# Marks that DVE and ACT write, turned into integer rows by GpSimd

## The chip, the cores and the metric

The program runs on one core of a Trainium2 chip. The metric is device time in microseconds (us) of one execution. The engines are PE (TensorE), DVE (VectorE), ACT (ScalarE), POOL (GpSimd) and SP (SyncE, which here only issues DMAs). Each engine works through its own queue in order. POOL both computes and issues the indirect DMAs, and while it issues one it can do nothing else.

## The reference

The input x has 4 x 2048 = 8192 tokens of 256 features. It is normalised (layernorm), and two branches work on the result. The first is a gated linear recurrence: a projection, a scan over time of an 8-wide state, and an output projection; it gives s. The second is a mixture of experts with 32 experts; it gives g. The result is x + s * silu(g). What matters here is how a token gets its place at an expert:

```python
scores = softmax(xf @ wg.T)                  # 32 experts in 8 groups of 4
# the best 4 groups are kept; of their experts the best K = 4 take the token
pos  = (jnp.cumsum(oh, axis=0) * oh).sum(-1) - 1     # its turn at that expert
keep = pos < cap                                     # cap = 1280 places an expert
dest = jnp.where(keep, fe * cap + pos, E * cap)
xe   = xp[buf_tok].reshape(E, cap, DIM)              # the rows that each expert gets
h    = silu(xe @ w1) * (xe @ w3);  out = (h @ w2) * buf_w
y    = zeros.at[buf_tok].add(out);  z = (silu(xf @ sw1) * (xf @ sw3)) @ sw2
g    = y + z
```

## The kernel before

**First stage: routing and shared work.** The tokens are taken in nine batches, r = 0 to 8: two of 512 tokens and seven of 1024. A batch lies in a tile `xt` of 128 partitions with 4 or 8 tokens on each. For each batch the kernel normalises it (`norm`), turns it by PE (`to_features`), computes the logits, picks the experts (`choose`), counts the places (`count`, `place`), and writes token number and weights beside the features (`weigh`). `place` leaves in the tile `t8` the row numbers, as floats, of each token's four places in a buffer `xd_d` in device memory. Between these steps lie the dense "shared" expert (`shared_hidden`, `shared_out`), the recurrence (`recur`, a scan on DVE in line 414) and its projection.

**Dispatch.** `dispatch(r, t8)` writes the rows as integers into a tile `put` and sends the tokens to their rows. It makes groups: 4 in batches 0 and 1, 8 in each later batch, 64 in all. A group is one small copy of 128 x 4 numbers from `t8` to `put` (line 595; the copy to another type is called a CAST in the profile), and behind it four indirect DMAs on POOL (`send`, line 546), each of which scatters 128 rows. The groups are not all emitted at once: they stand in the list `waiting`, and `go_on` emits one here and there among the other work, on DVE in most places (50 groups) and on ACT in some (14). In the last batch the groups go by column: the first two hold column 3 of all 1024 tokens, the next two column 2, and so on. A token's rows are sorted, so expert 0 can only be in column 3, expert 1 in columns 2 and 3, and so on.

**The order of the work.** The regions are under `manual_schedule(engines=engines)` with PE, DVE, ACT and SP: these four issue in the order in which the program emits. POOL is not among them. A planner orders POOL's queue, by what is ready in its own model and then by the order of emission.

**Second stage: the experts.** For each expert e, SP loads its rows from `xd_d` in tiles of 128 rows (`load_slots`, line 797, with a register load ahead of each); for experts 0 to 3 the first tile of each span waits for the scatters of the columns that can hold this expert (line 805 on). Rows go through PE (`turn`), `first_blocks`, `second_blocks`, then `hidden`, a seven-product scheme in which DVE writes the tile `h` in line 873 (its part `c`) and ACT in line 878; then `down` multiplies with w2, ACT scales (line 917) and POOL adds the rows to `y_d` by an indirect DMA (line 918). The two last blocks of the shared expert are written to `y_d` by POOL (line 619), the others by SP.

**Memory.** Tiles come from pools. `put` lies in the pool `keep`, which lives to the end. `t8`, with the rest of routing's small tiles, lies in the pool `rt`, two buffers of each name. The pools `ab`, `xp`, `rt` and `sh` of the first stage are given back at its end, and the second stage's pools `fin`, `moe`, `arms` and so on are laid from the same first byte. They are made with `reuse_waits="tile"`: a new tile waits for whoever still uses an earlier tile on its own bytes, and for nobody else. `h` is in `arms`.

**End.** The last stage loads `y_d`, applies silu, multiplies with s, adds x and writes the output.

Of the kernel before, what the change touches and what calls it, by code (L numbers as in the profile page):

```python
# [8 lines left out]
F32 = mybir.dt.float32  # L9
# [7 lines left out]
def recurrent_moe_kernel(  # L17
# [18 lines left out]
    nc = tc.nc  # L36
    P = 128
# [5 lines left out]
    K = 4  # L43
# [10 lines left out]
    RT = 8  # L54
# [72 lines left out]
    def go_on(n=1, copy=nc.vector.tensor_copy):  # L127
        for _ in range(min(n, len(waiting))):
            waiting.pop(0)(copy)
# [36 lines left out]
    with tc.tile_pool(name="ab", bufs=1) as ab, tc.tile_pool(name="xp", bufs=4) as xp, tc.tile_pool(  # L166
        name="rt", bufs=2
# [353 lines left out]
        def place(r, M, cum, pc):  # L521

            n = RTS[r]
            base = rt.tile([P, E], F32, tag="base", name=f"base_{r}")
            nc.vector.tensor_tensor(base, pc[:, 1, :], carry, ALU.add)
            nc.vector.tensor_tensor(carry, pc[:, 0, :], carry, ALU.add)
            ejs = [P, E, n]
            pos = by_expert("pos", r)
            nc.vector.tensor_tensor(pos, cum, base.unsqueeze(2).to_broadcast(ejs), ALU.add)
            over = by_expert("ml", r)  # L530
            nc.vector.tensor_scalar(over, pos, 0.0, 1.0e6, ALU.max, ALU.mult)
            nc.vector.tensor_tensor(pos, pos, eoff.unsqueeze(2).to_broadcast(ejs), ALU.add)
            nc.vector.tensor_tensor(pos, pos, over, ALU.add)
            sl = wide("sl", r)
            nc.vector.tensor_tensor(sl.rearrange("p j e -> p e j"), pos, M, ALU.mult)
            t8 = wide("t8", r, 8)
            for j in range(n):
                nc.vector.max(t8[:, j, :], sl[:, j, :])
            go_on(len(waiting))
            nc.vector.tensor_scalar(t8[:, :n, 0:K], t8[:, :n, 0:K], gone, None, ALU.min)  # L540
            return t8
# [3 lines left out]
        def send(index, rows, column):  # L545
            ins = nc.gpsimd.indirect_dma_start(  # L546
                out=xd_d,
                out_offset=bass.IndirectOffsetOnAxis(ap=index, axis=0),
                in_=rows,
                in_offset=None,  # L550
            )
            apart("xd", ins)
            sent.append((column, ins.ins.name))
            if column is not None:
                tc.add_to_no_dep_group(f"column{column}", ins.ins)
# [32 lines left out]
        def dispatch(r, t8):  # L588


            put = keep.tile([P, RT, K], I32, tag="put", bufs=2, name=f"put_{r}")
            final = r + 1 == NR

            def group(js, ks, copy):
                copy(put[:, js, ks], t8[:, js, ks])
                for j in range(js.start, js.stop):
                    for k in range(ks.start, ks.stop):
                        send(put[:, j, k : k + 1], xts[r][:, j, :], k if final else None)

            for i in range(RTS[r]):  # L600
                if final:
                    k, j = K - 1 - i // 2, i % 2 * K
                    waiting.append(lambda copy, a=slice(j, j + K), b=slice(k, k + 1): group(a, b, copy))
                else:
                    waiting.append(lambda copy, a=slice(i, i + 1): group(a, slice(0, K), copy))
            go_on(1 if 2 < r < NR - 1 else 2)
# [44 lines left out]
        put = place(0, M, cum, pc)  # L651
        weigh(0, M, ex)
        dispatch(0, put)
        load_x(3)
        gate_bias()
# [12 lines left out]
        put = place(1, M, cum, pc)  # L668
        weigh(1, M, ex)
        dispatch(1, put)  # L670
        load_x(4)
        to_features(2, 0, first=True)
# [14 lines left out]
        put = place(2, M, cum, pc)  # L687
        weigh(2, M, ex)
        dispatch(2, put)
        hT = shared_hidden(1)  # L690
        load_x(5)
# [17 lines left out]
        put = place(3, M, cum, pc)  # L709
# [14 lines left out]
        for r in range(4, NR + 1):  # L724
# [24 lines left out]
            if new:  # L749
                pc = count(r, cum)  # L750
                put = place(r, M, cum, pc)
# [374 lines left out]
```

## Time and profile before

| | |
|---|---|
| median of 3 runs | 1130.21 us (1129.55 to 1130.8) |
| profiled execution, its own time | 1130.25 us |
| span of its trace | 1128.4 us |
| PE busy | 1046.4 us of the span |
| POOL busy | 699.0 us |
| DVE busy | 700.1 us |
| ACT busy | 506.0 us |
| scatters of line 546 | 256, from 29.7 to 373.5 us |
| first row load of an expert (line 797) | 348.35 us |

The span runs from the first to the last instruction; 1.85 us of the execution lie around it. A line of the trace's timeline gives start, duration, engine, source line, operation, output and inputs, their shapes, and in brackets the idle time of the engine just before it and what ended it ("issue": nothing that the profile shows). A number such as x2 says that neighbouring instructions of one kind are merged. SPq, POOLq and so on are an engine's sequencer: it waits or issues, and the engine itself is idle.

### The profile page before, as it was taken

Reading aid. Unit: us, or ns where it says so; the run is one execution under the profiler, and the core shown is the slowest. Engines: PE = TensorE matmul, PEld = TensorE weight load, DVE = VectorE, ACT = ScalarE, POOL = GpSimd, SP = SyncE. Lnnn points to the kernel's source line nnn. Section 1 sums busy time; section 2 is a strip of 40 time slices with the busy share of each in tenths; the row PEclk is TensorE's granted clock in tenths of the full one; section 3 lists DMA queues with packets and bytes.
Section 4 is the critical chain, followed back from the end, with each engine's and each line's share of the span. In section 5 each row is a group of like instructions: output and inputs, shape, how many; then the busy total and the mean of one; then the engine's idle time right before and its main releaser. Section 6 shows DMA issues by size and latency. Waiting matters only on the chain.

```text
span 1128.4 us, 16045 instructions
## 1 busy us (share of the span) xinstructions
PE 1046.4 (93%) x3882; PEld 652.6 (58%) x3882; DVE 700.1 (62%) x1950; ACT 506.0 (45%) x990; POOL 699.0 (62%) x562
## 2 busy tenths in 40 slices
PE   6799899999999999999999999999999999999930
PEld 3366466566666566665566556665665665665620
DVE  6887786786542556555565555565555655655567
ACT  2355345534532444444444444444444444444442
POOL 2777777777777654566545655565566466466470
PEclk9999999999999999999999999999999999999975
DMA  6363443533368887777877887788777878778599
GB/s 212 125 204 124 166 156 135 186 132 146 130 207 260 211 192 155 156 143 182 173 169 161 167 204 164 135 175 192 148 153 171 188 157 190 170 148 166 99 255 388
DMA packets 149837, 197.28 MB, mean 175 GB/s; under 512 B 17706, under 2 KB 133331, under 8 KB 149715
## 3 DMA queue, kind: packets, MB, share of 16 engines
q0 software_dynamic: 53184, 79.07, 35.5%
q1 hardware_dynamic: 95922, 116.50, 34.1%
q8 instruction: 48, 0.79, 0.3%
q14 instruction: 75, 0.61, 0.2%
q10 hardware_dynamic: 608, 0.31, 0.1%
HBM read 99.05 MB, written 96.76 MB: 174 GB/s over the span
## 4 chain that ended last, share of the span: by engine, by line
PE 61%; DMA 2%; DVE 1%; issue 1%; POOL 0%; ACT 0%; SPq 0%; ACTq 0%; DVEq 0%; POOLq 0%
PE eo L915 20%; PE ps L867 19%; PE ps L870 14%; PE ep L842 5%; PE xu L102 3%; DMA out_dram<-xr 1%; DMA y<-y_d 1%; DVE y L1084 1%; PE xh L974 0%; PE xp L957 0%; DVE xr L1085 0%; POOL out_dram L1087 0%; POOL y_d L918 0%; ACT y L1083 0%; ACT ob L917 0%
## 5 line engine op out<-in xcount | busy, mean ns | idle before, releaser
L918 POOL DMA_INDIRECT y_d<-ob,row x274 | 424.0, 1547 | 293.5 <-DVE rf L816 200.4
L546 POOL DMA_INDIRECT xd_d<-xt,put x256 | 262.5, 1025 | 102.8 <-issue 61.5
L915 PE MATMUL eo<-w,h 128*128 128x256 f32 x1024 | 237.1, 379 | 0.3 <-DVE h L880 0.3
L915 PEld LDWEIGHTS eo<-w,h 128*128 128x128 f32 x1024 | 188.5, 190 | 31.3 <-issue 8.8
L917 ACT ACTIVATE ob<-eo,wt 128x256 f32<-128x256 f32 x274 | 118.9, 471 | 130.0 <-PE eo L915 130.0
L867 PE MATMUL ps<-B,S 128*128 128x512 f32 x384 | 175.3, 592 | 1.3 <-DVE B L858 1.3
L873 DVE TENSOR_TENSOR u<-p,ps 128x512 f32<-128x512 f32 x64 | 44.0, 687 | 186.6 <-PE ps L867 186.6
L870 PE MATMUL ps<-B,w 128*128 128x512 f32 x256 | 130.7, 592 | 0.0
L867 PEld LDWEIGHTS ps<-B,S 128*128 128x128 f32 x384 | 72.9, 190 | 93.4 <-issue 77.2
L893 ACT COPY ps<-v 128x512 f32<-128x512 f32 x64 | 37.7, 589 | 120.3 <-DVE v L873 120.3
L870 PEld LDWEIGHTS ps<-B,w 128*128 128x128 f32 x256 | 48.0, 189 | 61.9 <-DVE ps L873 31.2
L842 PEld LDWEIGHTS ep<-ident,xe 128*128 128x128 f32 x512 | 59.9, 141 | 20.2 <-DMA xe<-xd_d 9.8
L878 ACT ACTIVATE h<-ps 128x512 f32<-128x512 f32 x96 | 53.8, 595 | 30.7 <-PE ps L870 30.7
L102 PE MATMUL po<-Wio,xnT 128*128 128x256 f32 x256 | 66.8, 384 | 0.2 <-ACT zt L616 0.2
L842 PE MATMUL ep<-ident,xe 128*128 128x128 f32 x512 | 66.5, 273 | 0.3 <-ACT B L850 0.3
L867 PE MATMUL ps<-B,w 128*128 128x512 f32 x128 | 66.0, 597 | 0.6 <-DVEq L993 0.3
L870 PE MATMUL ps<-B,S 128*128 128x512 f32 x128 | 66.0, 598 | 0.1
L880 DVE TENSOR_TENSOR h<-h,ps 128x512 f32<-128x512 f32 x96 | 62.9, 682 | 3.3 <-PE ps L870 0.2
L102 PE MATMUL pz<-sw,hT_s 128*128 128x256 f32 x256 | 60.7, 390 | 0.4 <-DVE hT_s L142 0.4
L102 PE MATMUL pa_s<-xnT,sw 128*128 128x512 f32 x128 | 60.9, 598 | 0.0
L102 PE MATMUL pb_s<-xnT,sw 128*128 128x512 f32 x128 | 60.1, 592 | 0.0
L102 PEld LDWEIGHTS po<-Wio,xnT 128*128 128x128 f32 x256 | 48.4, 193 | 10.4 <-issue 3.8
(173 smaller groups left out, 1400.9 us busy)
## 6 DMA issues: line engine op xcount, KB each, us to landing
xe<-xd_d SPq DMA_DIRECT2D x320, 144.5 KB
w<-in_L_ffn_w_dram SPq DMA_DIRECT2D x96, 256.0 KB
xt<-in_L_attn_x_dram SPq DMA_DIRECT2D x16, 512.0 KB
xr<-in_L_attn_x_dram SPq DMA_DIRECT2D x16, 512.0 KB
y<-y_d SPq DMA_DIRECT2D x16, 512.0 KB
y_d<-zt SPq DMA_DIRECT2D x14, 512.0 KB
y_d<-ob,row POOLq DMA_INDIRECT x274, 4.9
xd_d<-xt,put POOLq DMA_INDIRECT x256, 2.7
```

Of the source, the lines that this page charges most:

```text
L102: nc.tensor.matmul(ps, lhsT, rhs, start=(i == 0), stop=(i == len(pairs) - 1))
L546: ins = nc.gpsimd.indirect_dma_start(out=xd_d, out_offset=bass.IndirectOffsetOnAxis(ap=index, axis=0), in_=rows, in_offset=None,)
L842: nc.tensor.transpose(ps[:, j * P : (j + 1) * P], xes[e, i][:, j, k * P : (k + 1) * P], ident)
L867: nc.tensor.matmul(ps[n], a, b, start=True, stop=True)
L870: nc.tensor.matmul(ps[n], a, b, start=False, stop=True, skip_group_check=True)
L873: nc.vector.tensor_tensor(to, a, b, ALU.add)
L878: nc.scalar.activation(h[:, m, t], src, AF.Silu)
L880: nc.vector.tensor_tensor(h[:, m, t], h[:, m, t], src, ALU.mult)
L893: nc.scalar.copy(ps[2], v)
L915: nc.tensor.matmul(po[:, i, :], hT(m), ws[e][:, 2, m, :], start=(m == 0), stop=(m == KH - 1))
L917: nc.scalar.activation(ob[:, q % 2, :], po[:, i, :], AF.Copy, scale=wts[e][:, q : q + 1])
L918: ins = nc.gpsimd.indirect_dma_start(out=y_d, out_offset=bass.IndirectOffsetOnAxis(ap=rows[e][:, q : q + 1], axis=0), in_=ob[:, q % 2, :], ...
```

## The change

`dispatch` gets a tile of floats, `mark`, from the pool `rt`. The copy that DVE or ACT makes for a group now goes from `t8` to `mark`, float to float. Behind it, POOL itself copies the group from `mark` to `put`, float to integer, and then issues the group's four scatters, which read `put` as before. The tile `put`, the scatters and all other work are the same.

```diff
@@ dispatch(r, t8)
             put = keep.tile([P, RT, K], I32, tag="put", bufs=2, name=f"put_{r}")
             final = r + 1 == NR
 
+            mark = rt.tile([P, RT, K], F32, tag="mark", name=f"mark_{r}")
+
             def group(js, ks, copy):
-                copy(put[:, js, ks], t8[:, js, ks])
+                copy(mark[:, js, ks], t8[:, js, ks])
+                nc.gpsimd.tensor_copy(put[:, js, ks], mark[:, js, ks])
                 for j in range(js.start, js.stop):
                     for k in range(ks.start, ks.stop):
                         send(put[:, j, k : k + 1], xts[r][:, j, :], k if final else None)
```

## The prediction

> **What bounds the kernel now.** I read the page's engine shares and chain first, then the busy table by stretches, then the timelines of POOL, SP, DVE and ACT around the change of stage.
>
> ```profile
> PE 1046.4 (93%) x3882; PEld 652.6 (58%) x3882; DVE 700.1 (62%) x1950; ACT 506.0 (45%) x990; POOL 699.0 (62%) x562
> 192.00:342.00 150.00, 143.55 (x552) 94.61 (x551) 96.67 (x398) 66.33 (x93) 115.88 (x112) 1.00 0.48 159
> 342.00:376.00 34.00, 32.04 (x112) 19.18 (x111) 11.91 (x22) 11.23 (x23) 24.77 (x27) 1.00 0.86 274
> ```
>
> The stretches list length, then PE, PEld, DVE, ACT, POOL. PE is full in both (143.55 of 150, 32.04 of 34), so POOL's 62% over the whole looks harmless. But POOL's own timeline says otherwise:
>
> ```profile
> 156.27 0.96 POOL L546 DMA_INDIRECT xd_d<-xt,put  x1 [0.30 <-issue]
> 158.67 1.27 POOL L546 DMA_INDIRECT xd_d<-xt,put  x1 [1.45 <-DVE put L595]
> 166.49 0.96 POOL L546 DMA_INDIRECT xd_d<-xt,put  x1 [1.72 <-DVE put L595]
> 192.31 0.95 POOL L546 DMA_INDIRECT xd_d<-xt,put  x1 [0.82 <-DVE put L595]
> 341.50 0.96 POOL L546 DMA_INDIRECT xd_d<-xt,put  x1 [0.30 <-issue]
> 367.83 0.59 POOL L619 DMA_DIRECT2D y_d<-zt  x1
> 368.73 0.99 POOL L546 DMA_INDIRECT xd_d<-xt,put  x1 [0.30 <-DVE h L873]
> ```
>
> A scatter lasts 0.96 and the next starts 0.30 later: one per 1.26 us, 5.05 a group. From 29.7 us to the end POOL really waits for a row copy in three places only, by 1.45, 1.72 and 0.82, of which 0.30 each is the usual gap: 3.1 us of slack. After 192.31 there is none: POOL's queue is a backlog, and whatever is added to it moves its end. The last copy is made by DVE at 353.78, its scatters start at 368.73, 15 us later. So the question is who waits for POOL around 340 to 380.
>
> ```profile
> 348.35 8.75 SPq L797 DMA_DIRECT2D xe<-xd_d  x8
> 353.78 0.17 DVE L595 CAST put<-t 128x4 int32<-128x4 f32 x1
> 367.95 0.69 DVE L873 TENSOR_TENSOR h<-v,ps 128x512 f32<-128x512 f32 x1 [0.17 <-PE ps L867]
> 368.81 0.60 ACT L878 ACTIVATE h<-ps 128x512 f32<-128x512 f32 x1 [0.35 <-PE ps L870]
> ```
>
> Here is expert 0's first load, which waits for column 3 (its last scatter is the 341.50 one), and the two first writes of `h`.
>
> **The price of a copy on POOL, c.** No row shows such a copy. The nearest are POOL's small operations at the start:
>
> ```profile
> 1.07 0.15 POOL L203 IOTA eoff<- 128x32 f32 x1
> 1.18 0.28 POOL masks.py:199 TENSOR_SCALAR_AFFINE_SELECT ident<-ident 128x128 f32<-128x128 f32 x1
> 1.43 0.28 POOL L199 TENSOR_SCALAR_AFFINE_SELECT tri<-tri 128x128 f32<-128x128 f32 x1
> 1.95 0.16 POOL L215 IOTA at<- 128x10 f32 x1
> 2.06 0.14 POOL L218 IOTA gone<- 128x1 f32 x1
> ```
>
> From below: short operations follow each other at 0.11 (1.95 to 2.06), less than their records, since they overlap. From above: the DMA of line 619 puts 0.59 between two scatters, and it is a whole DMA issue. Nearest is an operation that reads and writes, 0.25 from start to start for 128 numbers (1.18 to 1.43); for 4 numbers it must be nearer the short record of 0.16, but the scatter waits for its end, so nothing overlaps. I take 0.20. The 0.30 ahead of the scatter doesn't come twice: at 192.31 the scatter starts 0.28 after the end of the DVE copy that it waited for, as it would behind its own engine.
>
> A rule of the Trainium skill speaks against this change (SBUF — State Buffer, "SBUF: two separate sides"): DVE and GpSimd share one port pair as an exclusive lock, and a DVE operation with two SBUF inputs, or in a two-port mode, shuts a reading GpSimd operation out until it ends. The row first:
>
> ```profile
> 320.78 1.65 POOL L546 DMA_INDIRECT xd_d<-xt,put  x1 [0.30 <-issue]
> 322.74 2.02 POOL L546 DMA_INDIRECT xd_d<-xt,put  x1 [0.30 <-DMA xd_d<-hole]
> 321.64 2.34 DVE L414 TENSOR_TENSOR_SCAN St<-Gt,St,St 8x1024 f32<-8x1024 f32 x1
> ```
>
> While the scan runs, scatters take 1.65 and 2.02 in place of 0.96: the lock is real here. Were every DVE operation such a lock, a copy would meet one with 64% (96.67 of 150 us) and wait some 0.3 us for it (my estimate: mean operation 96.67 / 398 = 0.24, long ones are met more often), c would be 0.4 and the sum below +22. But all 256 scatters together are at a mean of 1.025 against 0.96, so the whole lock costs 0.065 for an operation five times as long; for a copy that is 0.01 to 0.07. I stay with 0.20.
>
> **Part by part.**
> 1. DVE's 50 and ACT's 14 copies stay: casts of 128x4 take 0.16 and 0.19, and the float copies nearest to them (line 813, 128x10 on DVE, 0.16; line 823, 128x4 on ACT, 0.19) the same. Zero. Their waits for `put` of two batches earlier (28 semaphore instructions on each of the two queues, 0.05 and 0.04 us) move to POOL, where the sequencer already takes 64 such during the scatter before without a gap over 0.30. Zero; without that cover 28 x 0.05 = 1.4 us on POOL. The waits on POOL that `mark` brings DVE and ACT are two batches (some 80 us) old.
> 2. POOL gets 64 x 0.20 = 12.8 us, all on its queue, and 3.1 of that falls into the three idle places. Behind each waiting copy stand all later scatters, the two stores of line 619 and expert 0's adds. Column 3 ends after 58 groups: 58 x 0.20 - 3.1 = **8.5 us later**. The last group's copy ends at 368.42 (the end of the store ahead of it) + 64 x 0.20 - 3.1 = **378.1**.
> 3. SP: the loads of `xt` wait for the scatters of four batches before. The last of them, at 205.49, comes 3 us later (32 groups: 6.4 - 3.1), but DVE first reads it at 247.21. The store queued behind it isn't due until 212.39. Zero, up to some 7 us.
> 4. Expert 0's load. From 341.50 to its issue at 348.35 it takes 6.85 us, where the median scatter lands 2.7 after its start: the DMA engines are full then with expert 0's weights, a store and the hole fills, which SP issues without asking POOL. 8.5 us later that crowd is gone, and I give 3.4 of it back. By the semaphore record expert 0's last tile lands at 360.82 and PE needs it at 362.09: 1.3 of slack. So this path costs 8.5 - 3.4 - 1.3 = **+3.8**.
> 5. `mark` has a place, and someone lies on it later. Counting the tiles' bytes per partition from the first byte of pool `ab`: `ab` and `xp` take 89,856, `rt`'s tiles up to the one before `mark` 15,232 more, so `mark` of batch 8 is at 105,088. In the second stage `fin`, `moe` and the two small row tiles of `arms` end at 104,352, and there begins `h`, 8192 bytes long. So `h` covers `mark`. Until now the last reader of rows on those bytes was DVE at 353.78, 14 us ahead of need. Now it is POOL's last copy, at 378.1, and the first write of `h` is due at 367.95 (DVE) or, if the wait is put on the part that covers it, 368.81 (ACT): 9.3 to 10.2 us late. PE stands behind it: ps is freed by these two.
>
> 4 and 5 are not added: both delay the same PE queue, and the later one decides. From there on PE is 97% busy to 1085 us (695.84 of 714 in 386 to 1100) and gives nothing back; about 0.3 of ACT's waits for late rows falls away. The sum: **+9.5**. On the profiled execution's own time, 1130.25 (span 1128.4 + 1.85), that is 1139.7; the median of the runs is 1130.21, 0.04 away, so 1139.7 for it too. In c: 64c - 3.1 - 0.2: +3.7 at 0.11, +12.7 at 0.25, +22 at 0.40, +35 at 0.60.
>
> **The rivals.**
> - *The planner moves copies forward.* It fills POOL's gaps: the IOTA at 1.07 was emitted after both selects and runs before them. If the last copy goes right behind the one of the group before, ahead of that group's scatters, it ends 5.7 us sooner, at 372.4, and part 5 asks only +4.4; further forward part 4 decides, +3.8. For: that row. Against: DVE makes these two marks 9.7 us apart, so the last is hardly ready in a plan that keeps up. 1134.3.
> - *Not slower.* The copies come in pairs, overlapped at 0.11 to 0.14, and early; then the column is late by 58 x 0.13 - 3.1 = 4.4, and the 3.4 and 1.3 of part 4 swallow it. The place is the first load of line 797; it decides below c = 0.14 if the last copy is at least two groups forward, otherwise only below c = 0.05. 1130.
> - *POOL pays more.* A copy has to wait for the scatter's drain, or the lock is worse than the mean tells: c = 0.35 gives +19, 1149. For: a copy stands alone between DMAs, which no row shows.
> - *A waiting copy blocks.* A copy put ahead of scatters that were ready waits for a late mark (DVE is just in time in three places); that adds up to 5 us: 1145. Part of the range.
>
> **How the numbers follow.** Likeliest, `h` waits for the last copy at c from 0.14 to 0.30: 57%, 1136 to 1146. Planner moves copies: 17%, 1133 to 1136. Costlier, or blocked: 14%, 1146 to 1160. Not slower, within 0.2% (2.3 us, about what a measurement here can tell): 8%. Faster, by a better fall of the scatters among DVE's scans (those cost POOL 16 us in all) or fewer waits on DVE: 4%. Slower thus 88%. The range leaves out some 12% below and 8% above: 1132.5 to 1150.
>
> **What would show it.** (Lines behind the change count 3 more.) 64 POOL copies of 128x4 at line 598, near 0.2; last scatter some 9.5 us later than 372.56; the first load of a row tile near 353.5; DVE's or ACT's first write of `h` waiting for POOL, and PE idle some 6 us there that it isn't now; after it the same 24 to 27 us an expert as now. I am wrong if `h` waits for something else, if the last copy stands before its neighbours' scatters, or if c is not near 0.2.

## The result, and the profile after

The changed kernel takes 1147.24 us at the median of four runs (1146.58 to 1153.08), the one before 1130.51 beside it (1129.55 to 1130.83): a ratio of **1.0164, interval 1.0151 to 1.0176** (the longest of the four runs draws it up; the medians alone give 1.0148). The change makes the kernel slower, as forecast, but by 16.3 us between the two profiled executions (1146.58 against 1130.25) where the sum said 9.5.

The page's first line, and the busy table by stretches (length, PE, PEld, DVE, ACT, POOL, then PE's granted clock, DMA share and GB/s), cut at 342 and 376 us; the third block is the last stretch in the kernel before.

```profile
PE 1052.6 (92%) x3882; PEld 656.5 (57%) x3882; DVE 701.4 (61%) x1950; ACT 507.1 (44%) x990; POOL 720.5 (63%) x626
```

```profile
192.00:342.00 150.00, 143.43 (x551) 94.52 (x550) 97.09 (x397) 66.17 (x91) 118.26 (x133) 1.00 0.44 153
342.00:376.00 34.00, 27.09 (x91) 16.78 (x90) 7.00 (x14) 7.16 (x13) 26.61 (x32) 0.85 0.68 218
376.00:402.00 26.00, 20.33 (x71) 12.23 (x70) 12.20 (x29) 9.53 (x24) 14.71 (x17) 0.87 0.63 183
```

```profile
376.00:402.00 26.00, 25.67 (x103) 16.77 (x102) 17.29 (x42) 11.92 (x29) 13.23 (x9) 1.00 0.81 187
```

Until 342 us PE does the same work in the same time (143.43 of 150, before 143.55). Then it is idle for 6.9 of 34 us and again for 5.7 of 26, where before these were 2.0 and 0.3, and its clock is no longer granted in full: 0.85 and 0.87 where before it was 1.00. POOL's share of the whole has moved by one point, from 62% to 63%.

The timeline of the changed kernel around the change of stage, with column 3's last scatter (353.65), expert 0's first load, POOL's last copy and the first writes of `h`:

```profile
353.50 0.17 DVE L597 COPY mark<-t 128x4 f32<-128x4 f32 x1
353.65 0.97 POOL L546 DMA_INDIRECT xd_d<-xt,put  x1 [0.31 <-issue]
...
354.63 0.20 POOL L598 CAST put<-mark 128x4 int32<-128x4 f32 x1
...
355.11 0.99 POOL L546 DMA_INDIRECT xd_d<-xt,put  x1 [0.28 <-POOL put L598]
...
357.45 1.73 SPq L800 DMA_DIRECT2D xe<-xd_d  x2
```

```profile
376.97 1.03 PE L873 MATMUL ps<-B,S 128*128 128x512 f32 x2
...
381.48 0.60 POOL L622 DMA_DIRECT2D y_d<-zt  x1
382.08 0.21 POOL L598 CAST put<-mark 128x4 int32<-128x4 f32 x1
382.32 0.60 ACT L881 ACTIVATE h<-ps 128x512 f32<-128x512 f32 x1 [5.50 <-POOL put L598]
382.32 0.69 DVE L876 TENSOR_TENSOR h<-v,ps 128x512 f32<-128x512 f32 x1 [6.18 <-POOL put L598]
382.56 1.01 POOL L546 DMA_INDIRECT xd_d<-xt,put  x1 [0.28 <-POOL put L598]
...
383.67 2.08 PE L873 MATMUL ps<-B,w 128*128 128x512 f32 x2 [5.67 <-DVE ps L876]
...
385.53 1.84 PE L870 MATMUL ps<-B,w 128*128 128x512 f32 x2
```

The same two pairs of products in the kernel before:

```profile
369.48 1.02 PE L870 MATMUL ps<-B,w 128*128 128x512 f32 x2
...
370.34 1.02 PE L867 MATMUL ps<-B,w 128*128 128x512 f32 x2
```

DVE made the last mark at 353.50, some 22 us before it stands ready to write `h` there: it is idle from 376.14. But POOL reads the mark at 382.08, at the end of its backlog. DVE and ACT, which write `h` over it, name that copy as what they waited for, 6.18 and 5.50 us, and start 0.03 us after it ends. PE waits behind them for 5.67 us, and its next two pairs of products take 2.08 and 1.84 where they took 1.02 each before.

Shifts against the profile of before, all from the timelines:

| | before, us | after, later by |
|---|---|---|
| last scatter of column 3 | 341.50 | 12.15 |
| expert 0's first load | 348.35 | 9.10 |
| first product of `hidden` | 362.79 | 8.33 |
| last group of scatters | 368.73 | 13.83 |
| first write of `h` | 367.95 | 14.37 |
| first product of `down` | 377.23 | 16.01 |
| end of the span | 1128.43 | 16.34 |

The loss is complete by 393 us; the 32 experts behind it keep their pace.

### The profile page after: what moved, and what is told of

It is laid out like the page before. It is cut to its first block, busy times and chain, and to the rows that moved or that the text cites. A ratio compares the mean times of both kernels' runs of the same rounds, so it can differ in the third digit from the quotient of the medians.

```text
span 1144.8 us, 16085 instructions
## 1 busy us (share of the span) xinstructions
PE 1052.6 (92%) x3882; PEld 656.5 (57%) x3882; DVE 701.4 (61%) x1950; ACT 507.1 (44%) x990; POOL 720.5 (63%) x626
## 4 chain that ended last, share of the span: by engine, by line
PE 63%; POOL 21%; issue 7%; DVE 6%; ACT 1%; DMA 1%; POOLq 0%; DVEq 0%; ACTq 0%
PE eo L918 21%; POOL xd_d L546 19%; PE ps L870 19%; PE ps L873 14%; PE ep L845 5%; PE xu L102 3%; DVE y L1087 2%; POOL put L598 1%; DVE xr L1088 1%; PE pz L102 1%; DMA xd_d<-xt,put 1%; DVE st L325 0%; DMA xt<-in_L_attn_x_dram 0%; ACT St L384 0%; PE xp L150 0%
## 5 line engine op out<-in xcount | busy, mean ns | idle before, releaser
L873 PE MATMUL ps<-B,w 128*128 128x512 f32 x256 | 131.8, 596 | 5.7 <-DVE ps L876 5.7
L845 PE MATMUL ep<-ident,xe 128*128 128x128 f32 x512 | 69.3, 277 | 6.1 <-DMA xe<-xd_d 6.1
L870 PE MATMUL ps<-B,w 128*128 128x512 f32 x128 | 67.5, 609 | 0.2
L859 DVE TENSOR_TENSOR B<-ep,B 128x512 f32<-128x512 f32 x32 | 22.1, 692 | 58.6 <-PE ep L845 38.6
```

The lines of the kernel that those rows point to most:

```text
L845: nc.tensor.transpose(ps[:, j * P : (j + 1) * P], xes[e, i][:, j, k * P : (k + 1) * P], ident)
L870: nc.tensor.matmul(ps[n], a, b, start=True, stop=True)
L873: nc.tensor.matmul(ps[n], a, b, start=False, stop=True, skip_group_check=True)
```

## The experiments

My theory going in was that `h` waits for POOL's last copy because it lies on `mark`, and that late rows for expert 0 cost about 8 us of their own, hidden below that wait. The rival was that POOL's backlog and the late rows cost it all, wherever the marks lie. Still open was why POOL's queue ended 4 us later than I had summed.

### The marks at another place

```diff
-            mark = rt.tile([P, RT, K], F32, tag="mark", name=f"mark_{r}")
+            mark = ab.tile([P, RT, K], F32, tag="mark", bufs=2, name=f"mark_{r}")
```

> The change whole, but the tile of marks comes from the pool ab instead of rt, so that h does not lie on it. If h's wait for the last POOL copy sets the price (my theory), h's first write waits for PE instead, and only the late load of expert 0 is left, which in the changed kernel was 8.3 us late: 1138 to 1140 us, 7 to 9 under the changed kernel, still about 8 to 9 over the one before. If POOL's backlog itself and the late rows set it, wherever the marks lie (rival): 1146 to 1148, as changed.

1138.62 us, ratio 1.0079 (1.0056 to 1.0102): half of the loss is gone by moving a tile of 128 bytes per partition. (The four runs fall into two pairs, 1136.6 and 1136.8, 1140.5 and 1141.3; the profile is of the one at 1136.8.)

```profile
354.84 9.64 SPq L800 DMA_DIRECT2D xe<-xd_d  x8
...
374.52 0.20 POOL L598 CAST put<-mark 128x4 int32<-128x4 f32 x1
...
374.73 0.69 DVE L876 TENSOR_TENSOR h<-v,ps 128x512 f32<-128x512 f32 x1 [0.17 <-PE ps L870]
...
375.59 0.60 ACT L881 ACTIVATE h<-ps 128x512 f32<-128x512 f32 x1 [0.34 <-PE ps L873]
...
380.40 0.21 POOL L598 CAST put<-mark 128x4 int32<-128x4 f32 x1
```

POOL's last copy is still late (380.40), but `h` is written at 374.73, 5.7 us before it, and waits for PE alone. The rival falls. What remains of the loss is the load: 6.5 us late (354.84), the first product 6.7, `h` 6.8, the span 6.65. (PE's own first stage ended 2.4 us late in this execution, behind a stretch at a granted clock of 0.5 from 327.65 to 331.06; but after it PE waits three times for expert 0's rows, up to 1.66 us, so the load decides.)

### The last group direct

```diff
+                if final and js.start and not ks.start:
+                    copy(put[:, js, ks], t8[:, js, ks])
+                else:
+                    copy(mark[:, js, ks], t8[:, js, ks])
+                    nc.gpsimd.tensor_copy(put[:, js, ks], mark[:, js, ks])
```

> The last group of all is copied by DVE or ACT straight to integers as before; the other 63 go by way of the marks. POOL's last copy is then that of group 63 of 64, one or two groups earlier in its queue, at about 376 instead of 382. My theory: h's first write follows it, 5 to 6 us earlier than in the changed kernel: 1140 to 1142 us. Rival (late rows, whatever the marks' place): one copy of 64 less, 0.2 us: 1146.5 to 1147.

1140.11 us (1136.83 to 1142.88), ratio 1.0081 (1.0054 to 1.0107): one copy of 64 left out brings 7 us between the medians, 5.6 between the profiled executions.

```profile
376.56 0.20 POOL L601 CAST put<-mark 128x4 int32<-128x4 f32 x1
...
378.42 0.69 DVE L879 TENSOR_TENSOR h<-v,ps 128x512 f32<-128x512 f32 x1 [0.23 <-PE ps L873]
```

The size is as expected, the reason not wholly. POOL's last copy ends at 376.76, and `h` no longer waits for it: its first write, at 378.42, waits for PE, which is late by its rows (load +9.8, first product +10.0). The load path takes over as soon as the copy is out of the way.

### The last batch alone, and all but the last batch

The same condition, with `if not final` (only batch 8 goes by way of the marks) and with `if final` (only batches 0 to 7 do).

> Only batch 8 (8 groups) goes by way of the marks; batches 0 to 7 as before. My theory: POOL gets 8 copies at 0.24, 1.9 us, and h waits for the last of them at about 368.7 + 1.7 = 370.4 where it was due at 367.95 to 368.8: +1.7 to +2.5, so 1132 to 1133 us; column 3 is 0.5 us late, which the load's slack takes. Rival (the whole backlog's lateness): 1.9 of 13.8 us, so 1130.5 to 1132.5, and no write of h that waits for POOL. If the scatters are 12 ns longer for the whole program because a POOL copy is in it, all 256 last 0.972 and the last group is 4 to 5 us late in place of 1.9: 1135.

1131.76 us, ratio 1.0015 (1.0007 to 1.0023). Eight copies are enough to make `h` wait for POOL, though they add next to nothing to its backlog (the last group is 0.7 late):

```profile
368.99 0.21 POOL L601 CAST put<-mark 128x4 int32<-128x4 f32 x1
369.23 0.69 DVE L879 TENSOR_TENSOR h<-v,ps 128x512 f32<-128x512 f32 x1 [2.71 <-POOL put L601]
369.23 0.60 ACT L884 ACTIVATE h<-ps 128x512 f32<-128x512 f32 x1 [2.03 <-POOL put L601]
```

So batch 8's copies alone bring the wait; what the other 56 add to POOL's queue sets its length (`h` +1.3 here, +14.4 in the changed kernel). PE's wait of 2.20 us did not slow its clock: its next pairs took 1.13 and 1.02. And the scatters stayed at 0.960 at the median, behind the copies too; the first one after each copy takes 0.98.

> Batches 0 to 7 (56 groups) go by way of the marks, batch 8 straight to integers as before. No copy of POOL's is left behind column 3, and h's first write cannot wait for one of batch 8. My theory: column 3 is still about 11.5 us late, expert 0's first load some 8 to 9, its first matmuls about 8: 1137.5 to 1139.5 us. That would be the price of the late rows alone. If the late rows cost what the changed kernel lost (rival): 1145 to 1147. If they are hidden: 1130 to 1131.

1140.52 us, ratio 1.0080 (1.0060 to 1.0101), about 1 us over what I expected: the late rows alone. The first load is 10.2 us late and so is the first write of `h`, which waits for PE; the span is 10.7 longer. POOL's last copy ended at 339.66. In this kernel the scatters of batch 8, which have no copies among them, still last 0.969.

### POOL's time alone

```diff
+            spare = ab.tile([P, RT, K], F32, tag="spare", bufs=2, name=f"spare_{r}")
...
                 copy(put[:, js, ks], t8[:, js, ks])
+                nc.gpsimd.tensor_copy(spare[:, js, ks], put[:, js, ks])
```

> DVE and ACT write integers as before, and POOL makes, at the place of its copy, another one from the integer rows to a tile of floats that nobody reads (64 copies as in the change, but no scatter reads what they write). This is the price of POOL's time alone. If what POOL pays is the copy's time, its gap and longer scatters: the last group of scatters is 12 to 14 us late as in the changed kernel, no write of h waits for POOL, and the time is 1138 to 1140 us. If the price came of the hand-over (scatter waits for POOL's own copy): the copies hide in the 0.30 ahead of the scatters, the last group is under 7 us late, and the time is 1130 to 1134.

1133.51 us, ratio 1.0024 (1.0013 to 1.0035). I expected 1138 to 1140, and was wrong: the last group is 6.7 us late, not 13.8, and the first load 3.1. POOL's timeline in a quiet stretch, first of this kernel, then of the changed one:

```profile
211.66 0.97 POOL L546 DMA_INDIRECT xd_d<-xt,put  x1 [0.30 <-issue]
212.63 0.19 POOL L598 CAST spare<-put 128x4 f32<-128x4 int32 x1
212.99 0.98 POOL L546 DMA_INDIRECT xd_d<-xt,put  x1 [0.17 <-issue]
```

```profile
213.14 0.97 POOL L546 DMA_INDIRECT xd_d<-xt,put  x1 [0.30 <-issue]
214.12 0.20 POOL L598 CAST put<-mark 128x4 int32<-128x4 f32 x1
214.59 0.99 POOL L546 DMA_INDIRECT xd_d<-xt,put  x1 [0.28 <-POOL put L598]
```

Both copies start where the scatter ends and last 0.2. Behind a copy that it doesn't need, the next scatter starts after 0.17; behind the one that it reads, after 0.28; two scatters in a row are 0.30 apart. So a copy by itself puts 0.06 us on the queue here and 0.18 in the changed kernel (medians); on the mean, with the few copies that take far longer (below), 0.11 and 0.235. More than half of the queue's price is not the copy but the hand-over.

### Every copy twice

```diff
+            spare = ab.tile([P, RT, K], I32, tag="spare", bufs=2, name=f"spare_{r}")
...
                 copy(mark[:, js, ks], t8[:, js, ks])
+                nc.gpsimd.tensor_copy(spare[:, js, ks], mark[:, js, ks])
                 nc.gpsimd.tensor_copy(put[:, js, ks], mark[:, js, ks])
```

> As changed, and one more POOL copy of the same 128x4 per group from the marks to a tile that nobody reads; 128 copies in all. My theory: every further copy puts 0.11 (overlapped with the other, as short POOL operations follow each other at the start) to 0.27 us (alone, with DVE's lock) on the queue, so h's first write comes 7 to 17 us later than in the changed kernel: 1154 to 1164 us. That gives the slope of the time in the price of a copy: 1 us for each us that POOL's last copy is later. If h's wait is not what decides, the slope is under a half: 1147 to 1151.

1154.35 us, ratio 1.0206 (1.0186 to 1.0225). The second of two neighbouring copies starts 0.13 after the first (208.50 and 208.63), so 64 of them make 8 us; the last copy ends 8.0 us later (390.29) and `h` starts 8.0 later:

```profile
390.09 0.20 POOL L600 CAST put<-mark 128x4 int32<-128x4 f32 x1
...
390.32 0.69 DVE L878 TENSOR_TENSOR h<-v,ps 128x512 f32<-128x512 f32 x1 [8.59 <-POOL put L600]
```

The time grows by 7.1 between the medians and by 9.55 between the profiled executions. Within that spread, and with `h` itself 8.0 for 8.0, nothing absorbs it: once `h` waits, a microsecond on POOL's queue is about one in the time.

### Which scatters become longer

In the changed kernel the scatters last 0.972 at the median in place of 0.960, and the shortest 0.968 in place of 0.954: 256 x 0.012 = 3.1 us that I had not foreseen. In the kernel with the last batch alone they lasted 0.960, even behind copies. There POOL's first scatter ran before its first copy, so I tried the order.

```diff
+                if r == 0 and js.start == 0:
+                    copy(put[:, js, ks], t8[:, js, ks])
+                else:
+                    copy(mark[:, js, ks], t8[:, js, ks])
+                    nc.gpsimd.tensor_copy(put[:, js, ks], mark[:, js, ks])
```

> As changed, but the first group of all (batch 0) is copied by DVE straight to integers, so that POOL's first scatters run before its first copy; 63 groups as changed, marks in the same place. Where POOL's copies came first, every scatter of the program lasted 0.97 instead of 0.96; where all scatters' kind was first met ahead of the first copy (only batch 8 changed), they lasted 0.96 even behind copies. If it is the order of first use (theory): scatters at 0.960 throughout, the last group about 2.5 us less late than in the changed kernel, h follows it: 1143 to 1145.5 us. If it is the number of copies, or anything else of the change (rival): scatters at 0.970 to 0.972 and 1146 to 1148 us.

Against it, the kernel before with one copy in front of its first scatter (only for `r == 0` and the first group, to a tile `spare`):

> As before the change, with one single copy of 128x4 on POOL ahead of the first scatters, to a tile that nobody reads. Order of first use (theory): all 256 scatters last 0.970, 10 ns each, the last group is 2.5 us late less what the idle places take, and the load's landing takes that: 1130 to 1132 us. Rival: the single copy is gone after 0.2 us, scatters stay at 0.960, 1129.5 to 1131 us.

The scatters' group by line, with shortest, median and longest in ns: of the changed kernel, of the one with 63 copies but the first group direct, and of the kernel before with one copy in front.

```profile
L546 POOL DMA_INDIRECT xd_d<-xt,put x256: 968/972/2854, 30.2 to 386.4; - x128
```

```profile
L546 POOL DMA_INDIRECT xd_d<-xt,put x256: 956/960/2848, 29.3 to 383.1; - x128
```

```profile
L546 POOL DMA_INDIRECT xd_d<-xt,put x256: 965/969/2013, 30.0 to 373.0; - x128
```

63 copies and no lengthening; one copy, 340 us before the last scatter, and the shortest of all 256 is above the median of before. It is not the number of copies but what POOL ran ahead of its first scatter. The kernel with the first group direct takes 1143.54 us, ratio 1.0107 (1.0089 to 1.0125), 3.7 under the changed kernel: its last copy ends at 378.94 in place of 382.29. Not all of that is the scatters' length, as the next part shows. The single copy costs nothing that can be measured, ratio 1.0006 (0.9997 to 1.0015): the scatters' records sum to 3.1 more up to the last group, but 3.0 of it falls into the places where POOL was idle before, and the last group is only 0.4 late.

Two more kernels ask whether it takes a copy. Before the first scatters of the kernel before ran one addition (`tensor_tensor`) of two 128x4, and in the next kernel that addition and the copy.

> As before the change, with one single POOL addition of two 128x4 ahead of the first scatters, to a tile that nobody reads. If any kind of POOL operation that is met ahead of the scatters lengthens them: 0.970 at the median. If only a copy does: 0.960. The time says nothing here: 1129 to 1132 us.

> As before the change, with one POOL addition and one POOL copy of 128x4 ahead of the first scatters, to a tile that nobody reads. If each kind met earlier adds its own 10 ns: scatters at 0.980 at the median. If it is one step, taken once: 0.970. 1129 to 1133 us.

```profile
L546 POOL DMA_INDIRECT xd_d<-xt,put x256: 965/969/2011, 29.3 to 372.6; - x128
```

```profile
L546 POOL DMA_INDIRECT xd_d<-xt,put x256: 956/960/2012, 30.0 to 371.7; - x128
```

One addition: 0.969, as with one copy. An addition and then a copy: 0.960, as with neither, which I had not expected at all. An even number is not what does it: in the changed kernel two copies run ahead of the first scatter (0.972), with every copy twice four (0.969). So the lengthening follows which operations ran before the first scatter. Why, these runs do not show, and the last two kernels ran once each. Their times, 1130.9 and 1130.95, lie in the spread of the kernel before.

### Both mended

The marks in pool `ab`, and the first group direct.

> The change with two things mended: the marks come from the pool ab, so that h does not lie on them, and the first group of all goes straight to integers, so that the scatters' kind is met ahead of the first copy. If the parts add up as I now think: scatters at 0.960, column 3 some 8.9 us late, expert 0's first load some 4.7 and its first products 3.3 us late, no write of h that waits for POOL, and no half clock behind it: 1133 to 1135 us. If the shorter scatters bring nothing once h is out of the way: 1138 to 1139, as with the marks' place alone.

1134.44 us, ratio 1.0041 (1.0027 to 1.0055). The scatters' median is 0.961, the first load 3.7 us late, the first product 3.0, `h` 3.2 and without a wait for POOL:

```profile
371.12 0.69 DVE L879 TENSOR_TENSOR h<-v,ps 128x512 f32<-128x512 f32 x1 [0.17 <-PE ps L873]
```

The parts add up: 1138.62 with the marks elsewhere, less the 3.7 of the first group, makes 1134.9. It is still slower than before the change, and nothing in these runs points to a version that is faster: POOL's copies only lengthen a queue that had no slack left after 192 us.

## Why the prediction was right in its direction and short by 7 us

**The copies of DVE and ACT** (step 1) are at zero as said: DVE's 50 casts have a median of 0.164, its 50 copies too, ACT's 14 have 0.194, and PE's first stage ends 0.28 us sooner than before. Of the waits for a place, 5 of DVE's 28 and 2 of ACT's are left; one of ACT's took 1.6 us.

**The price c** of one undisturbed copy was right: 0.199 at the median where I took 0.20, and the gap ahead of the scatter is 0.28, as said. **The lock** of the Trainium skill that I weighed (SBUF — State Buffer, "SBUF: two separate sides") fits the copies' rows too, and came out at the upper end of my 0.01 to 0.07, which I then left out of c: 64 copies sum to 16.95 us, 4.2 over 64 x 0.199, which is 0.066 each. DVE and POOL in the changed kernel:

```profile
240.49 2.34 DVE L414 TENSOR_TENSOR_SCAN St<-Gt,St,St 8x1024 f32<-8x1024 f32 x1
...
241.29 1.52 POOL L598 CAST put<-mark 128x4 int32<-128x4 f32 x1
```

The copy starts within the scan and ends with it, at 242.81 and 242.83. Six of the 64 copies take over 0.3 us, each until such a DVE operation with two inputs ends; the others don't, though DVE is busy 64% of the time. The 0.4 that the rule would have given if all of DVE's work locked was far off. (Of the two long scatters that I showed for the lock, the first ran mostly under the DVE operation ahead of the scan, line 412 from 320.39 to 321.61, and ended while the scan still ran; each of the two ends 0.8 us after the DVE operation that it met.)

**POOL's queue** (step 2) is the first step that failed, in its size: 64 copies at 0.20 less 3.1 of idle places made 9.7 us for the last group and 8.5 for column 3; measured are 13.83 and 12.15. POOL's records from the first scatter to the last group show where the rest went (the rows add up to within 0.03):

| us | summed | changed | first group direct |
|---|---|---|---|
| first scatter later than at 29.70 | 0 | 0.49 | -0.42 |
| put on the queue by the copies | 12.8 | 14.52 | 13.98 |
| scatters' records longer than before, in sum | 0 | 1.85 | 0.00 |
| idle places used up | -3.1 | -3.06 | -3.09 |
| last group later | 9.7 | 13.83 | 10.48 |

So 1.7 of the missing 4.1 lies in the copies, 1.85 in the scatters, 0.5 in the start. The copies come near 12.8 by two errors that in part cancel: a copy puts only 0.18 on the queue, and four pairs no more than one copy each, so that 58 places make 10.4; the copies that meet DVE add 4.1. The scatters were put at nothing: 252 of them, 0.012 longer each, make 3.0, but in this execution they waited 1.2 less for DVE. The kernel with the first group direct, in which they are not longer, comes within 0.8 of the forecast. Yet that it is the length alone is not shown. With the marks elsewhere, the first group direct brings the last group forward by about as much, 3.06 us, but there the scatters' sum falls by 0.08 only, the copies' by 1.9, and the first scatter starts 1.0 sooner.

**Expert 0's load** (step 4): forecast 8.5 - 3.4 - 1.3 = 3.8; measured 12.15 - 3.05 - 0.77 = 8.33. The landing did come back by about 3 us, the slack was 0.8 in place of 1.3; what was wrong is the first term. In the kernel with the first group direct the same path gives 3.25. Where this path decides, it lengthens the span by 6.7 (marks elsewhere) to 10.7 (all but the last batch), as a loss of its own, not added to the other.

**The wait of `h`** (step 5) is as described, down to the line: both writers name POOL's copy, and the later of steps 4 and 5 decides. The forecast's 9.3 to 10.2 became 14.37: DVE's own 10.2 and the 4.2 of the copy's end. That PE idles 5.67 us where I said some 6 is luck: its rows and the copy both came over 4 us later than summed, and the difference stayed.

**What I left out** is the second step that failed. "From there on PE gives nothing back" put what follows the wait at nothing; it takes something more. Between the first write of `h` and the first product of `down` the changed kernel loses another 1.64 us, because PE comes back at half its clock (2.08 and 1.84 for a pair of products in place of 1.02). The granted clock, the third figure from the end, is 0.51 there and 1.00 behind it:

```profile
383.60:387.20 3.60, 3.53 (x4) 1.52 (x5) 0.01 (x1) 1.16 (x3) 2.71 (x3) 0.51 0.93 309
387.20:393.00 5.80, 5.80 (x19) 2.77 (x18) 4.29 (x7) 1.50 (x5) 0.79 (x2) 1.00 0.31 125
```

The loss comes with the longer waits only:

| kernel | PE's wait before the first pair behind `h`, us | that pair, then the next, us | lost between `h` and `down`, us |
|---|---|---|---|
| last batch alone | 2.20 | 1.13, 1.02 | -0.08 |
| changed | 5.67 | 2.08, 1.84 | 1.64 |
| first group direct | 6.32 | 2.08, 1.92 | 1.87 |
| every copy twice | 8.09 | 2.08, 1.92 | 2.32 |

In three kernels in which `h` waits for PE alone (marks elsewhere, last group direct, all but the last batch) this stretch takes 9.22 to 9.28 us, as before the change (9.28). An earlier stretch at half clock in the changed kernel, 363.27 to 373.51, behind the wait for expert 0's rows, adds nothing behind the first product: that and the next group of products are both 8.3 late.

This is what the Trainium skill describes (TensorE: Matmul & The Clock Gate, "Part 1: The HAM clock gate"): a TensorE that has been idle runs at half clock until about 3.4 us of activity release it. The traces agree: a wait of 2.20 us left the clock full, waits of 5.67 and more halved it, and in the last three kernels of the table it is granted in full again 3.5 to 4.9 us after PE's restart. At half clock for 3.4 us, PE does 1.7 us of work less; that is an estimate from the page, and the traces' 1.6 to 2.3 stand beside it. I had the idle time of 6 us in my text and did not ask what the engine's clock does behind it.

The sum put right, on the profiled executions: 9.5, plus 0.65 for DVE's own lateness in place of a middle between DVE and ACT, plus 4.2 for the last copy's end, plus 1.64 for the clock, plus 0.33 until the end of the span, makes 16.3.

**The rivals.** The planner did put several copies next to the one before them, but not the last, which stands behind a store. No copy waited for a mark except the first of all. "POOL pays more" came nearest in time (1149 at c = 0.35) and would have been taken for right by the time alone. It has a part in it: with the waits for DVE a copy lasts 0.265 on the mean and puts 0.235 on the queue. But the undisturbed copy is 0.20, and no copy waited for a scatter's drain: the copies start 0.01 after a scatter's end. The time lies 1.2 above the band that I gave to the wait of `h`, 1136 to 1146.

## What to carry to other kernels

A tile's last reader sets when its bytes come free: giving a read to an engine with a backlog of 15 us holds the place for those 15 us more, and whatever the next stage lays there waits, however small the tile is. Look at who is put on the bytes before costing the instruction, and choose the pool by that. When a sum ends in a wait of several microseconds on TensorE, add the restart at half clock (1.6 to 2.3 us here, behind waits of 5.7 to 8.1); and when an operation is given to a queue that is full, count what it does to its neighbours' durations and gaps (on the mean 0.11 us a copy that nobody waits for, 0.235 one that the next scatter reads), not its own length alone.

## What the hardware showed that I had not expected

- A scatter on POOL takes 0.960 or 0.969 to 0.972 us at the median of the whole program, depending on which operations POOL ran ahead of the first one: 0.969 to 0.972 behind one, two or four copies, 0.969 behind one addition, 0.960 behind neither, or behind an addition and a copy. Over 256 scatters that is 2.3 to 3.1 us; how much of it reaches the end of the queue differs from kernel to kernel. The cause is open.
- A POOL copy of 128x4 that met one of DVE's scans or its other long operations with two inputs lasted until that ended, up to 1.52 us for 0.20 of work. In the changed kernel it happened to 6 copies of 64.
- A scatter starts 0.17 us behind a copy that it doesn't need, 0.28 behind the copy that it reads, and 0.30 behind another scatter.
